# Moving a bank read to another engine, and two residual sums to later places, in a kernel bound by TensorE

## The chip, the cores and the metric

The kernel runs on one core of a Trainium2 chip. The metric is the device time of one execution in microseconds, the median of several runs. Looks of one run: of those, only places are compared. The five instruction streams are TensorE (PE), VectorE (DVE), ScalarE (ACT), GpSimd (POOL) and the DMA issuing queue (SP).

## The reference

A graph attention net on 128 graphs of 64 tokens with 768 features, two layers, in float32:

```python
h = jnp.maximum(_layernorm(x, axis=-1), 0.0)
for l in range(2):
    m_left  = einsum('bsh,oh->bso', h, W_left[l]);  m_right = einsum('bsh,oh->bso', h, W_right[l])
    u_left  = einsum('bih,bjh->bij', h, m_left) / sqrt(768);  u_right = ... m_right ...
    u = u_left * upper_triangle(adj) + u_right * lower_triangle(adj)     # cut: how the masks are made
    e = exp(u) * adj
    attention = e / (sum(e, axis=2) + 1e-10)
    h_lin = einsum('bsh,oh->bso', h, W_lin[l]) + b_lin[l]
    h = relu(layer_norm(attention @ h_lin, ln_a[l], ln_b[l]))
return x + h
```

## The kernel before

The work goes through 16 blocks of 512 tokens. Each 768x768 projection is cut into blocks of 256 and done with 15 block products instead of 18, of sums of token blocks (`ts`) and sums of weight blocks. A product is made in one of the PSUM banks X, Y, Z, V and added to one or two of six output blocks in `hl` (three of 256 columns, for two halves of the tokens), with a sign; further products then accumulate **on top of it in the same bank**. So a bank must be read before the next matmuls of that bank may start: a late read stops TensorE, in the profile of before for 0.45 us at one read and 1.07 at another.

```python
# product i: (weights, bank, tokens, what it is added to)
ORDER = ((5, "X", "ta", "+2"), (8, "Z", "u1", "-0+2"), (0, "X", "u2", "+3"), (1, "Y", "u3", "-3"),
         (12, "X", "B3", "-5"), (6, "V", "B0", "-2"), ...                       # cut
         (3, "X", "u0", "+1-3"), (11, "Y", "te", "+0"), (13, "V", "tc", "-1"), (9, "Z", "tg", "+4"),
         (14, "V", "tf", "+5"))

def read(p, to, i, seen):
    what = ORDER[i][3]
    for n in range(0, len(what), 2):
        sign, o = what[n], int(what[n + 1])
        if o not in seen:                     # first time for this output: a copy, on ScalarE
            seen.add(o)
            nc.scalar.activation(to(o), p, AF.Copy, scale=1.0 if sign == "+" else -1.0)
        else:                                 # else an addition, on VectorE
            added(nc.vector, to(o), sign, to(o), p)
```

Other work is put at numbered slots of the loop over the products: slots 2i and 2i+1 come before and after the read of product i. The place of an instruction in its own engine's queue is fixed by that; nothing else is. The last block goes through the products twice, for one half of the tokens each. In its first half stand the final sums of the half-block before:

```python
def last_block(u):                                                         # cut
    put(1, lambda: load(1))                                                # rows of x, by DMA
    put(6, lambda: nc.gpsimd.tensor_scalar_mul(rows["-b"], rows["b"], -1.0))
    put(20, lambda: load(0))
    for xs, slot in zip(XS[u, 1], (22, 40)):                               # "offset sums": x + b
        put(slot, lambda xs=xs: nc.gpsimd.tensor_add(xs, xs, rows["b"]))

def finish(u, r):                                                          # cut
    # scaled(k): normalise on VectorE, then the "bias sum" on GpSimd
    nc.gpsimd.tensor_add(zs[k], zs[k], rows["b"])
    # done(k): the "residual sum" on VectorE, then the output
    nc.vector.scalar_tensor_tensor(xs[k], zs[k], 0.0, xs[k], op0=ALU.max, op1=ALU.add)

# slots of (inverse, scaled 0, scaled 1, done 0, done 1), for the two half-blocks before
ends = ({0: ((u - 1, 0), (12, 13, 15, 19, 21)), 9: ((u - 1, 1), (28, 29, 30, 39, 41))}, ...)
```

I call the product on "u0" (bank X), the start of the part of interest, **T**: after it come Y, V, Z and the last V group.

The softmax here doesn't subtract the row's maximum and nothing guards it: scores larger than these inputs give would overflow.

Of the kernel before, what the change touches and what calls it, by code (L numbers as in the profile page):

```python
# [17 lines left out]
def kernel(  # L18
# [24 lines left out]
    nc = tc.nc  # L43
# [33 lines left out]
    def put(slot, *fs):  # L77
        plan.setdefault(slot, []).extend(fs)

    def put_all(slot, fs, step=1):  # L80
        for f in fs:
            if f is not None:
                put(slot, f)
            slot += step
        return slot

    def run(slot):
        if slot in plan:
            for f in plan.pop(slot):
                f()  # L90
        elif idle:
            f = idle.popleft()
            if f is not None:
                f()
# [59 lines left out]
    def added(eng, o, sign, a, b):  # L154
        (eng.tensor_add if sign == "+" else eng.tensor_sub)(o, a, b)  # L155
# [13 lines left out]
    def tokens_of(key):  # L169
        ht = HT[key]  # L170
        r = {f"B{2 * j + t}": ht[:, j * K2:(j + 1) * K2, t * TH:(t + 1) * TH] for j in range(3) for t in range(2)}
        r.update(TS.get(key, {}))
        return r
# [12 lines left out]
    def put_sums_t(key, first, step, base):  # L186

        fs = sums_t(key)
        put_all(first, fs[:5], step)
        for f, s in zip(fs[5:], (21, 22, 23, 24, 25, 27)):  # L190
            put(max(base + s, first + 5 * step), f)

    def read(p, to, i, seen):

        what = ORDER[i][3]
        for n in range(0, len(what), 2):
            sign, o = what[n], int(what[n + 1])
            if o not in seen:
                seen.add(o)
                nc.scalar.activation(to(o), p, AF.Copy, scale=1.0 if sign == "+" else -1.0)  # L200
            else:
                added(nc.vector, to(o), sign, to(o), p)
# [60 lines left out]
    def load_h(which, l, u):  # L263
        ht = HT[which, l, u] = big.tile([P, C, T], F32, name="ht")
        nc.sync.dma_start(ht, KEPT[l][u])

    def affine(which, l, u, step=1):

        def part(c0):
            for c in range(c0, c0 + step):  # L270
                ht = HT[which, l, u][:, c, :]
                nc.scalar.activation(ht, ht, AF.Relu, bias=cols[1][:, c:c + 1], scale=cols[0][:, c:c + 1])  # L272

        return [lambda c=c: part(c) for c in range(0, C if l else 0, step)]
# [336 lines left out]
    def fresh(l, i, rs):  # L611

        bank = ps_st.tile([P, 2 * TH], F32, name=FIRST[i][0])
        b = bank.rearrange("p (r d) -> p r d", r=2)[:, :len(rs)]
        if i in PRELOAD:
            nc.scalar.copy(b, rows["bias", l][:, PRELOAD[i]].unsqueeze(1).to_broadcast([P, len(rs), D]))
        return b


    def pass_two(l, aside):  # L620
        last = l == L - 1
        with tc.tile_pool(name=f"two{l}", bufs=2, reuse_waits="tile") as sp:
# [8 lines left out]
            def load_at(u):  # L631
                AT[u] = sp.tile([P, Q, S], F32, name="at", bufs=2)
                nc.sync.dma_start(AT[u], ATT[l][u])
# [37 lines left out]
            def batch(r, k, h):  # L671
                return 4 * (h if k == 0 else 1 - h) + r + 2 * k

            XS = {}

            def last_block(u):


                rest = big.tile([P, C, T], F32, name="ht").rearrange("p c t -> p (c t)")
                rows["-b"] = sp.tile([P, H], F32, name="nb", bufs=1)  # L680
                for r in range(2):
                    XS[u, r] = [rest[:, n * H:(n + 1) * H] for n in (2 * r, 2 * r + 1)]

                def load(r):
                    for k in range(2):
                        for h in range(PAIR):
                            nc.sync.dma_start(XS[u, r][k][h * S:(h + 1) * S], x[u * NBB + batch(r, k, h)])

                put(1, lambda: load(1))
                put(6, lambda: nc.gpsimd.tensor_scalar_mul(rows["-b"], rows["b"], -1.0))  # L690
                put(20, lambda: load(0))
                for xs, slot in zip(XS[u, 1], (22, 40)):
                    put(slot, lambda xs=xs: nc.gpsimd.tensor_add(xs, xs, rows["b"]))

            def finish_last(u, r):
# [120 lines left out]
            def linear(u, rs, base, ends, more):  # L816

                b, w = tokens_of((2, l, u)), W[l, "n"]
                if rs[0] == 0:
                    HL[u] = sp.tile([P, Q, H], F32, name="hl", bufs=2)  # L820
                hl, seen = HL[u], set()
                bank = {"X": AHEAD.pop()}
                early = {0: 3, 2: 5, 6: 9}
                for i, (s, at, t, _) in enumerate(ORDER):
                    if i in FIRST and i not in PRELOAD:
                        bank[at] = fresh(l, i, rs)
                    p = bank[at]
                    for n, r in enumerate(rs):
                        for c in range(K2):
                            nc.tensor.matmul(p[:, n], b[t][:, c, r * P:(r + 1) * P], w[s][:, c, :],  # L830
                                             start=(i in FIRST and i not in PRELOAD and n == c == 0),
                                             stop=(c == K2 - 1), skip_group_check=True)
                        if n == 0:
                            run(base + 2 * i)
                    read(p, lambda o: hl[:, o % 2 * 2 + rs[0]:o % 2 * 2 + rs[0] + len(rs), o // 2 * D:(o // 2 + 1) * D],
                         i, seen)
                    if i in early:
                        bank[FIRST[early[i]][0]] = fresh(l, early[i], rs)
                    if i == 11 and more and 12 not in ends:
                        AHEAD.append(fresh(l, 0, more))  # L840
                    if i in ends:
                        what, slots = ends[i]
                        if slots:
                            for f, n in zip(finish(*what), slots):
                                put(n, f)
                        else:
                            finish_block(what, more)
                    run(base + 2 * i + 1)
# [3 lines left out]
            for u in range(NB):  # L852
                turn = not last and u >= NB - 2
                put(4, lambda u=u: load_at(u))
                if u + 1 < NB:
                    load_h(2, l, u + 1)
                    put_all(9 if u else 15, affine(2, l, u + 1))
                    put_sums_t((2, l, u + 1), 15 if u else 21, 1, 0)
                    if turn:
                        load_rows(1, 0, sp)  # L860
                        put_all(10, transpose_rows(1, 0, sp), 2)
                    if u in aside:
                        aside[u]()
                    ends = {}
                    if u and last:
                        ends = {0: ((u - 1, 0), (6, 7, 8, 11, 12)), 7: ((u - 1, 1), (20, 21, 22, 30, 30))}
                    elif u > NB - 3:
                        ends = {5: ((u - 1, 0), (16, 17, 18)), 11: ((u - 1, 1), (28, 29, 30))}
                    elif u:
                        ends = {12: (u - 1, None)}  # L870
                    linear(u, (0, 1), 0, ends, (0, 1) if u + 2 < NB else (0,))
                    for n in sorted(plan):
                        plan[n - 30] = plan.pop(n)
                else:
                    if turn:
                        load_h(1, 1, 0)
                        put_all(28, affine(1, 1, 0), 3)
                        put_sums_t((1, 1, 0), 38, 2, 30)
                        ends = ({1: ((u - 1, 0), (13, 14, 16)), 11: ((u - 1, 1), (34, 35, 36))},
                                {4: ((u, 0), (50, 51, 52))})  # L880
                    else:
                        last_block(u)
                        ends = ({0: ((u - 1, 0), (12, 13, 15, 19, 21)), 9: ((u - 1, 1), (28, 29, 30, 39, 41))},
                                {2: ((u, 0), (44, 48, 51, 61, 62))})
                    linear(u, (0,), 0, ends[0], (1,))
                    linear(u, (1,), 30, ends[1], ())
                    for n in sorted(plan):
                        run(n)
                    for f in (finish_last if last else finish)(u, 1):
                        f()  # L890
# [48 lines left out]
```

## Time and profile before

| | before |
|---|---|
| median of the first three runs | 2760.3 us (2755.51 to 2762.19) |
| span of the profiled run | 2755.1 us |
| TensorE busy | 2726.7 us, 99% |
| TensorE's own waits together | about 18 us, 8.9 of them at the start |
| first layer, last block: "u2" group to the V group after "B3" | 3.41 us (2.69 at its own pace) |
| second layer, last block: T to the end of the last matmul | 23.0 us |

A row of a timeline has its start, its duration, the engine, the source line, the operation, output and inputs and their shapes, and in brackets the idle time before it and who ended it. Starts of TensorE's groups are more telling than durations, since matmuls overlap: groups of four, 1.03 us long, start 0.86 us apart at its own pace.

### The profile page before, as it was taken

What the parts mean: (1) busy time and instruction counts of PE and PEld (TensorE: products, weight loads), DVE (VectorE), ACT (ScalarE), POOL (GpSimd) and SP (SyncE); (2) the same over time, 40 slices, a digit from 0 to 9 for tenths busy, and PEclk for the clock granted to TensorE, in tenths of its full rate; (3) what the DMA queues carried; (4) which work ended last, traced back from release to release, by engine and by line L of the source; (5) the groups of instructions that cost most, each with busy time, mean ns of one, the idle gap of its engine ahead of it and who ended that gap; (6) DMA issues with size and microseconds to landing.
All of it is one profiled execution on the core that took longest, in us unless ns stands there. A gap on an engine that the chain in (4) does not pass through costs nothing.

```text
span 2755.1 us, 46372 instructions
## 1 busy us (share of the span) xinstructions
PE 2726.7 (99%) x18712; PEld 2339.0 (85%) x18712; DVE 1349.0 (49%) x2268; ACT 850.0 (31%) x1612; POOL 1192.1 (43%) x935
## 2 busy tenths in 40 slices
PE   8999999999999999999999999999999999999998
PEld 7888888888888888888788888888888888888886
DVE  6455455545454333333335444444444335676667
ACT  3222223222221154444621211121122214444443
POOL 3432352224223555555522344223222325887885
PEclk9999999999999999999999999999999999999999
DMA  6534433343332333343555433443344204555655
GB/s 195 129 75 97 121 83 81 86 120 94 76 77 75 102 105 119 119 150 123 148 127 149 101 75 76 108 118 79 76 98 120 59 26 145 160 170 166 175 161 146
DMA packets 234072, 310.82 MB, mean 113 GB/s; under 512 B 54146, under 2 KB 184450, under 8 KB 225666
## 3 DMA queue, kind: packets, MB, share of 16 engines
q1 hardware_dynamic: 233698, 307.45, 41.7%
q8 instruction: 149, 2.44, 0.4%
q14 instruction: 65, 0.53, 0.1%
q10 hardware_dynamic: 160, 0.39, 0.0%
HBM read 202.91 MB, written 104.86 MB: 112 GB/s over the span
## 4 chain that ended last, share of the span: by engine, by line
PE 96%; DVE 1%; DMA 1%; ACT 1%; issue 0%; SPq 0%; DVEq 0%; ACTq 0%
PE X L426 23%; PE V L426 16%; PE X L830 12%; PE Y L426 12%; PE Z L426 8%; PE V L830 8%; PE Y L830 6%; PE aux L453 5%; PE Z L830 4%; PE aux L645 2%; PE aux L668 1%; PE Y L668 0%; ACT ht L272 0%; DMA w_r<-in_w_right_dram 0%; DMA ht<-h 0%
## 5 line engine op out<-in xcount | busy, mean ns | idle before, releaser
L155 POOL TENSOR_TENSOR ts<-ht 128x512 f32<-128x512 f32 x441 | 586.8, 1340 | 1223.1 <-DMA ht<-h 531.1
L200 ACT ACTIVATE m<-X 128x512 f32<-128x512 f32 (+1 forms) x256 | 151.6, 592 | 1086.4 <-PE X L426 570.7
L155 POOL TENSOR_TENSOR ts<-ht,ts 128x512 f32<-128x512 f32 x189 | 248.8, 1323 | 135.1 <-PE X L830 60.5
L155 DVE TENSOR_TENSOR m<-m,V 128x512 f32<-128x512 f32 (+1 forms) x256 | 173.3, 677 | 269.4 <-PE V L426 269.2
L155 DVE TENSOR_TENSOR m<-m,X 128x512 f32<-128x512 f32 (+1 forms) x256 | 162.9, 677 | 249.3 <-PE X L426 248.7
L830 PE MATMUL X<-w_n,ts 128*128 128x256 f32 x1024 | 244.3, 380 | 0.9 <-ACT hl L200 0.6
L426 PE MATMUL X<-ts,w_l 128*128 128x256 f32 x1024 | 242.7, 380 | 0.1
L426 PE MATMUL X<-ts,w_r 128*128 128x252 f32 (+1 forms) x1024 | 238.7, 376 | 0.0
L155 DVE TENSOR_TENSOR m<-m,Z 128x512 f32<-128x512 f32 (+1 forms) x128 | 87.5, 683 | 306.5 <-ACT m L200 246.9
L830 PEld LDWEIGHTS X<-w_n,ts 128*128 128x128 f32 x1024 | 191.4, 190 | 33.4 <-issue 3.7
L426 PEld LDWEIGHTS X<-ts,w_l 128*128 128x128 f32 x1024 | 191.9, 190 | 30.2 <-DVE m L155 2.7
L426 PEld LDWEIGHTS X<-ts,w_r 128*128 128x128 f32 x1024 | 191.9, 190 | 26.1
L272 ACT ACTIVATE ht<-ht,b_col,a_col 128x512 f32<-128x512 f32 x192 | 143.6, 804 | 149.3 <-DMA ht<-h 149.3
L830 PE MATMUL Y<-w_n,ts 128*128 128x256 f32 x768 | 182.5, 379 | 0.0
L426 PE MATMUL Y<-ts,w_l 128*128 128x256 f32 x768 | 181.5, 379 | 0.5 <-DVE w_l L155 0.5
L426 PE MATMUL Y<-ts,w_r 128*128 128x252 f32 (+1 forms) x768 | 179.2, 376 | 1.3 <-POOL w_r L155 1.3
L426 PEld LDWEIGHTS Y<-ts,w_l 128*128 128x128 f32 x768 | 145.8, 190 | 20.7 <-DVE w_l L155 0.9
L830 PEld LDWEIGHTS Y<-w_n,ts 128*128 128x128 f32 x768 | 145.8, 190 | 20.4 <-issue 0.6
L426 PEld LDWEIGHTS Y<-ts,w_r 128*128 128x128 f32 x768 | 145.8, 190 | 19.1 <-POOL w_r L155 1.7
L155 DVE TENSOR_TENSOR hl<-hl,V 128x512 f32<-128x512 f32 (+1 forms) x136 | 89.1, 655 | 129.7 <-PE V L830 112.4
L200 ACT ACTIVATE hl<-X 128x512 f32<-128x512 f32 (+1 forms) x136 | 78.3, 576 | 221.4 <-PE X L830 218.6
L796 POOL TENSOR_TENSOR z<-z,b 128x768 f32<-128x768 f32 x62 | 112.0, 1817 | 79.7 <-DVE z L793 79.7
(162 smaller groups left out, 4730.9 us busy)
## 6 DMA issues: line engine op xcount, KB each, us to landing
ht<-h SPq DMA_DIRECT2D x63, 1536.0 KB, 7.2
h<-xb SPq DMA_DIRECT2D x124, 384.0 KB, 6.1
z<-z SPq DMA_DIRECT2D x128, 192.0 KB, 3.1
x<-z SPq DMA_DIRECT2D x128, 192.0 KB, 8.6
x<-in_x_dram SPq DMA_DIRECT2D x120, 192.0 KB, 8.6
xr<-in_x_dram SPq DMA_DIRECT2D x120, 192.0 KB, 3.7
out_dram<-xr SPq DMA_DIRECT2D x120, 192.0 KB, 2.7
adj<-in_adj_dram SPq DMA_DIRECT2D x64, 128.0 KB, 2.8
```

The source lines that it names most:

```text
L155: (eng.tensor_add if sign == "+" else eng.tensor_sub)(o, a, b)
L200: nc.scalar.activation(to(o), p, AF.Copy, scale=1.0 if sign == "+" else -1.0)
L272: nc.scalar.activation(ht, ht, AF.Relu, bias=cols[1][:, c:c + 1], scale=cols[0][:, c:c + 1])
L426: nc.tensor.matmul(p[:, g], w[ORDER[i][0]][:, c, g * P:(g + 1) * P], b()[t][:, c, :].rearrange(bs, s=S)[:, :, :ns], start=(new and g == c ...
L453: nc.tensor.matmul(p[h * S + e:h * S + e + 32, q, e:e + 95], ht[:, c, b * S + e:b * S + e + 32], mb[:, e:e + 95], start=(c == 0), stop=(c ...
L645: nc.tensor.matmul(cx[k][i, m, :HH], at[j, q, :], hl[j, q, m * HH:(m + 1) * HH], start=True, stop=True)
L668: nc.tensor.matmul(parts[r, k][n][i], at[j, q, :], hl[j, q, cut], start=True, stop=True)
L796: nc.gpsimd.tensor_add(zs[k], zs[k], rows["b"])
L830: nc.tensor.matmul(p[:, n], b[t][:, c, r * P:(r + 1) * P], w[s][:, c, :], start=(i in FIRST and i not in PRELOAD and n == c == 0), stop=(c ...
```

## The change

The intent is to take away two stops of TensorE: the read of "u2" in the last block of the first layer goes from a busy ScalarE to an idle VectorE, and in the last block the residual sums go to later slots, so that they do not stand ahead of the reads of X, with the offset sums on GpSimd put behind them.

```diff
-    def read(p, to, i, seen):
+    def read(p, to, i, seen, copied=nc.scalar):
@@
                 seen.add(o)
+                if copied is nc.vector:
+                    nc.vector.tensor_scalar_mul(to(o), p, 1.0 if sign == "+" else -1.0)
+                    continue
                 nc.scalar.activation(to(o), p, AF.Copy, scale=1.0 if sign == "+" else -1.0)
@@ last_block
-                for xs, slot in zip(XS[u, 1], (22, 40)):
+                for xs, slot in zip(XS[u, 1], (26, 45)):
@@ linear
-                         i, seen)
+                         i, seen, nc.vector if (len(rs), rs[0], i) == (1, 0, 2) and not last else nc.scalar)
@@
-                        ends = ({0: ((u - 1, 0), (12, 13, 15, 19, 21)), ...
+                        ends = ({0: ((u - 1, 0), (12, 13, 15, 22, 24)), ...
```

The changed kernel has three more source lines: L200, L693, L796, L807, L830 of before are L203, L696, L799, L810, L833 there. The new read is L201.

More of the change, by code (lines that the diff above doesn't have):

```diff
@@ L882, in pass_two @@
                         last_block(u)
-                        ends = ({0: ((u - 1, 0), (12, 13, 15, 19, 21)), 9: ((u - 1, 1), (28, 29, 30, 39, 41))},
+                        ends = ({0: ((u - 1, 0), (12, 13, 15, 22, 24)), 9: ((u - 1, 1), (28, 29, 30, 39, 41))},
                                 {2: ((u, 0), (44, 48, 51, 61, 62))})
```

## The prediction

"Lock", here and in the expectations, is the word for what the durations show and for nothing more: the residual sum on VectorE took 0.94 us with GpSimd idle and 2.42 and 1.91 us when a sum on GpSimd was running, and ended some 0.82 us after that one.

> **What bounds the kernel now.** I read the page's busy shares first, then the chain that ended last, then the list of TensorE's own waits, and last the timelines of two short stretches.
>
> ```profile
> PE 2726.7 (99%) x18712; PEld 2339.0 (85%) x18712; DVE 1349.0 (49%) x2268; ACT 850.0 (31%) x1612; POOL 1192.1 (43%) x935
> PE 96%; DVE 1%; DMA 1%; ACT 1%; issue 0%; SPq 0%; DVEq 0%; ACTq 0%
> ```
>
> TensorE is busy 99% of the span and carries 96% of the chain that ended last. Busy matmul time alone would be a weak argument, but the starts are evenly spaced: groups of four 128x256 matmuls begin 0.86 to 0.87 us apart all through the trace, so between the gaps there is nothing for another engine to take away. What can be won is the time in which TensorE stands still for somebody, and that is listed:
>
> ```profile
> PE aux L347 <- ACT x L297: 8.9, 1, 8.9
> PE X L426 <- DVE w_l L155: 1.5, 1, 1.5
> PE Y L426 <- POOL w_r L155: 1.3, 1, 1.3
> ...
> PE V L830 <- DVE hl L155: 1.1, 1, 1.1
> PE X L830 <- ACT hl L200: 1.0, 3, 0.5
> ```
>
> Columns: who waited for whom, us in total, times, longest. Everything here is some 18 us, half of it the start-up. The change addresses two entries: the 1.1 us for one VectorE read of bank V, and the largest of the three waits for a ScalarE read of bank X. The first is in the last block of the second layer, the second in the last block of the first layer. The first layer's place:
>
> ```profile
> 1348.23 1.03 PE L830 MATMUL Y<-w_n,ts 128*128 128x256 f32 x4
> 1349.71 1.13 PE L830 MATMUL X<-w_n,ht 128*128 128x256 f32 x4 [0.45 <-ACT hl L200]
> ...
> 1348.16 0.81 ACT L783 ACTIVATE z<-aux 128x768 f32<-128x768 f32 x1
> ...
> 1349.29 0.36 ACT L200 ACTIVATE hl<-X 128x256 f32<-128x256 f32 x1
> ```
>
> The product "u2" (begun at 1347.26, finished about 1348.39) lies in bank X, and the matmuls on "B3" go on top of it, so it must be read first. The reader is ScalarE, which is busy with two row-square sums and a root until 1349.38; TensorE stands from 1349.26. The second layer's place, VectorE first, then GpSimd, then TensorE:
>
> ```profile
> 2720.62 2.42 DVE L807 SCALAR_TENSOR_TENSOR xr<-z,xr 128x768 f32<-128x768 f32 x1
> 2722.97 0.74 DVE L155 TENSOR_TENSOR hl<-hl,X 128x256 f32<-128x256 f32 x2
> 2723.63 1.91 DVE L807 SCALAR_TENSOR_TENSOR xr<-z,xr 128x768 f32<-128x768 f32 x1
> 2725.46 0.41 DVE L155 TENSOR_TENSOR hl<-hl,Y 128x256 f32<-128x256 f32 x1
> 2725.79 0.41 DVE L155 TENSOR_TENSOR hl<-hl,V 128x256 f32<-128x256 f32 x1
> ...
> 2718.65 3.58 POOL L796 TENSOR_TENSOR z<-z,b 128x768 f32<-128x768 f32 x2 [0.27 <-DVE z L793]
> 2722.78 1.94 POOL L693 TENSOR_TENSOR ht<-ht,b 128x768 f32<-128x768 f32 x1 [0.55 <-DMA ht<-in_x_dram]
> ...
> 2726.35 1.10 PE L830 MATMUL V<-w_n,ts 128*128 128x256 f32 x4 [1.07 <-DVE hl L155]
> ```
>
> The same residual sum (L807) takes 2.42, then 1.91 us here, and 0.94 us where GpSimd is idle (the one at 2735.41). Each long one ends about 0.82 us after a GpSimd sum does: the second bias sum ends at 2722.23, the residual sum at 2723.05; the offset sum (L693) ends at 2724.72, the residual sum at 2725.54. And the offset sum itself took 1.94 instead of 1.82, having started while the first residual sum was running. So the two engines exclude each other. The read of V comes behind both residual sums, and TensorE pays.
>
> [...] the reads of banks X, Y and V take 0.41 us under a running GpSimd sum as well as without. [...]
>
> **The change part by part.** The instruction order of the two kernels, compared engine by engine, differs in few places. TensorE and GpSimd have the same instructions in the same order with the same kinds of wait. ScalarE loses one read and VectorE gains one (first layer). In the last block VectorE's order goes from "sum, X, X, sum, Y, V, Z" to "X, X, sum, Y, sum, V, Z". On the DMA queue the second load of residual rows moves ahead of an output.
>
> 1. First layer's read on VectorE. VectorE has been idle since about 1346.75, so it can begin when bank X is done, about 1348.4. I take 0.42 us for it, as for its other 128x256 reads: free at about 1348.8. TensorE's next start at its own pace is 1348.23 + 0.86 = 1349.09, so the wait goes entirely. Worth: 1349.71 - 1349.09 = 0.62 us, and the group after a stop takes 0.96 to the next start (1350.67) instead of 0.86, which is 0.10 more. Sum: -0.72 us. Later waits in that block are for things that TensorE itself paces (reads of banks made just before), so they move along and give nothing back.
>
> 2. Offset sums "behind". GpSimd's queue is unchanged: bias sum, bias sum, offset sum, in that order. The first offset sum waits only for its rows (idle 0.55 us, ended by the DMA). A later place in the program does not hold it, since no other instruction stands between on GpSimd and it waits on nothing of VectorE. It should start at about 2722.78 as before, on before's clock, and so should the second, behind the two bias sums. Worth: 0.
>
> 3. Residual sums later. On before's clock. The reads of X wait for their matmuls (2721.56 + 1.13 = 2722.69), begin at about 2722.75 and end two starts of 0.33 later, at 2723.4. The first residual sum now comes up at 2723.4 with the offset sum holding the lock since 2722.78, for 1.82: until 2724.6. It ends 0.82 later, at 2725.42. Y: issued at 2725.34, the next start 0.33 later. Second residual sum from 2725.67, lock free, 0.94: next start about 2726.53. The read of V therefore begins at 2726.53, where it began at 2725.79: +0.74. TensorE started V 0.56 after the read began (2726.35 - 2725.79); it now starts at about 2727.09. Worth: +0.74 us. All of that is on the path, because the rest of this block, the last context and the closing chain of VectorE hang on TensorE's pace.
>
> The loss follows from one plain fact: before, the first residual sum spent its lock wait in time when VectorE had nothing else to do (X was not yet ready). Moved behind X, it meets the offset sum instead, while the second sum still stands ahead of V.
>
> 4. Earlier load of rows: they are used some 20 us later. Worth: 0.
>
> Sum: -0.72 + 0 + 0.74 + 0 = about 0.0 us of 2755.
>
> **The rivals.** (a) What the change is meant to do: if the offset sum fell behind both residual sums, they would take 0.94 each: 2723.4, Y, 2724.6, V at about 2725.5, and TensorE's stop shrinks by some 0.3 us; with step 1 about -1 us. With the stop gone altogether (own pace 2724.25 + 0.86 = 2725.11, so 1.24 + 0.1) it is -2 us. Against it: GpSimd's unchanged order and waits. For it: the load could land later, as more loads follow it closely. (b) The residual sum wins the lock and the offset sum comes between it and the second one: 2723.4 to 2724.3, offset sum to about 2726.0, second sum to 2726.85, V at 2726.8: +1.0 instead of +0.74, in all +0.3 us. It needs the rows to land 0.6 us later than before. (c) The moved read in the first layer delays VectorE's other reads. [...] the next one (Y) waited until 1349.69 in any case, for ScalarE's read; it will come earlier. I give that little weight. All rivals lie within -2 to +1 us, under a tenth of a percent.
>
> **Range and chances.** The three timed runs before lie 6.7 us apart (2755.51 to 2762.19, median 2760.3), and the profiled one took 2756.92. That scatter is larger than every branch above. So I predict 2760.0 us, with 2755 to 2764 for 8 in 10, that is the scatter of before plus the branches. 2% would be 55 us, and all waits of TensorE together are some 18: faster 0.005, same 0.99, slower 0.005.
>
> **What would show it.** Step 1: TensorE's 0.45 us wait before the "B3" matmuls of the first layer's last block is gone and the bank X read stands on VectorE at about 0.4 us. Step 2: GpSimd's first offset sum begins right after its rows land, not behind the residual sums. Step 3: the first residual sum shows about 2.0 us, the second about 0.95, and TensorE's stop before the last V group grows from 1.07 to about 1.8 us. It is wrong if that stop shrinks, if the offset sum starts after 2724, or if another wait of TensorE over 0.3 us appears. The time as a whole would be wrong only if a new wait repeated in all blocks, and nothing changes in them.

## The result, and the profile after

The changed kernel took 2758.66 us (median of 4 runs, 2756.18 to 2759.05), the kernel before 2758.3 (median of 4, the three above and one more). The ratio is 0.9998 with a 95% interval from 0.9981 to 1.0016: the same. A ratio is the mean time of one kernel's runs over that of the other's of the same rounds, so not quite the ratio of the medians. Busy times hardly differ:

```profile
PE 2726.2 (99%) x18712; PEld 2339.2 (85%) x18712; DVE 1347.4 (49%) x2269; ACT 849.5 (31%) x1611; POOL 1192.3 (43%) x935
```

TensorE's waits (us in total, times, longest) show what this hides. The 0.45 us wait for ScalarE's read is gone; the one that the second part was made for has doubled:

```profile
PE aux L350 <- ACT x L300: 8.6, 1, 8.6
PE V L833 <- DVE hl L155: 2.1, 1, 2.1
PE X L833 <- ACT X L619: 1.7, 1, 1.7
...
PE X L833 <- ACT hl L203: 0.6, 2, 0.3
```

The first layer's place in the changed kernel, TensorE, then VectorE:

```profile
1347.66 1.03 PE L833 MATMUL Y<-w_n,ts 128*128 128x256 f32 x4
1348.53 1.03 PE L833 MATMUL X<-w_n,ht 128*128 128x256 f32 x4
...
1347.86 0.42 DVE L201 TENSOR_SCALAR hl<-X 128x256 f32<-128x256 f32 x1 [1.68 <-PE X L833]
```

The read (L201) takes 0.42 us on VectorE after 1.68 us of idleness, and "B3" starts at TensorE's pace, 0.87 us after the group before it, where it was 1.48. And the last block, VectorE, GpSimd, TensorE:

```profile
2723.98 0.95 DVE L810 SCALAR_TENSOR_TENSOR xr<-z,xr 128x768 f32<-128x768 f32 x1
2724.85 0.41 DVE L155 TENSOR_TENSOR hl<-hl,Y 128x256 f32<-128x256 f32 x1
2725.18 2.23 DVE L810 SCALAR_TENSOR_TENSOR xr<-z,xr 128x768 f32<-128x768 f32 x1
2727.34 0.41 DVE L155 TENSOR_TENSOR hl<-hl,V 128x256 f32<-128x256 f32 x1
...
2724.51 2.09 POOL L696 TENSOR_TENSOR ht<-ht,b 128x768 f32<-128x768 f32 x1 [1.76 <-DMA ht<-in_x_dram]
...
2724.77 1.03 PE L833 MATMUL Z<-w_n,ts 128*128 128x256 f32 x4
2727.89 1.10 PE L833 MATMUL V<-w_n,ts 128*128 128x256 f32 x4 [2.10 <-DVE hl L155]
```

The first residual sum came up 1.91 us after T (2722.07) and found GpSimd idle: 0.95 us. But the offset sum began 2.44 us after T, in the middle of it, and so stood first in line when the second residual sum came up at 3.11 us. That one waited for the end of the offset sum (2726.60) and ended 0.81 us later. The read of V, behind it, started 1.55 us later than in the kernel before on the common clock, or 1.04 after allowing for the different T. Why the offset sum began so much later than before (1.23 us after T there) is not told by one trace.

The third line of the waits, 1.7 us, is new too. It lies at the start of the second layer's second pass and hangs on the landing of a 1.5 MB load; in the fourteen profiles, this wait was between 0.16 and 1.73 us, and 0.16, 0.23 and 1.55 for three looks at one and the same program. It is scatter, and no part of the change.

### The profile page after: what moved, and what is told of

Read it like the earlier page. It is cut to its first block, busy times and chain, and to the rows that moved or that the text cites. A ratio compares the mean times of both kernels' runs of the same rounds, so it can differ in the third digit from the quotient of the medians.

```text
span 2756.7 us, 46373 instructions
## 1 busy us (share of the span) xinstructions
PE 2726.2 (99%) x18712; PEld 2339.2 (85%) x18712; DVE 1347.4 (49%) x2269; ACT 849.5 (31%) x1611; POOL 1192.3 (43%) x935
## 3 DMA queue, kind: packets, MB, share of 16 engines
q8 instruction: 149, 2.44, 0.4%
## 5 line engine op out<-in xcount | busy, mean ns | idle before, releaser
L203 ACT ACTIVATE m<-X 128x512 f32<-128x512 f32 (+1 forms) x256 | 151.5, 592 | 1086.0 <-PE X L429 570.1
L833 PE MATMUL X<-w_n,ts 128*128 128x256 f32 x1024 | 244.3, 380 | 2.5 <-ACT X L619 1.7
L833 PEld LDWEIGHTS X<-w_n,ts 128*128 128x128 f32 x1024 | 191.5, 190 | 35.0 <-issue 3.1
L833 PE MATMUL Y<-w_n,ts 128*128 128x256 f32 x768 | 182.5, 379 | 0.0
L833 PEld LDWEIGHTS Y<-w_n,ts 128*128 128x128 f32 x768 | 145.8, 190 | 20.4 <-issue 0.6
L203 ACT ACTIVATE hl<-X 128x512 f32<-128x512 f32 (+1 forms) x135 | 77.9, 577 | 222.2 <-PE X L833 219.3
L799 POOL TENSOR_TENSOR z<-z,b 128x768 f32<-128x768 f32 x62 | 111.9, 1816 | 79.4 <-DVE z L796 79.4
```

Of the source, the lines that this page charges most:

```text
L833: nc.tensor.matmul(p[:, n], b[t][:, c, r * P:(r + 1) * P], w[s][:, c, :], start=(i in FIRST and i not in PRELOAD and n == c == 0), stop=(c ...
```

## The experiments

My theory: the two parts are independent, each worth what it does to one local wait; in the last block all that counts is whether GpSimd is in the middle of a sum when a residual sum comes up (0.94 us if not, 1.9 to 2.4 if so, in the profile of before). Rivals: the moved read costs something later; the order of loads or the offset sums' places matter; the stop is due to the mere number of sums ahead of V.

Each kernel was profiled once. From each trace I took five starts, and worked out: the distance from the Z group to the last V group (0.86 at TensorE's pace), the start of the offset sum after T, the durations of the two residual sums, the time from T to the end of the last matmul, and the time at half clock in between. Behind the last matmul every kernel needs another 10.5 to 10.6 us.

| run | first-layer read | sums | Z to V | offset sum after T | residual sums | T to last matmul | half clock |
|---|---|---|---|---|---|---|---|
| before | ScalarE | old | 2.10 | 1.23 | 2.42, 1.91 | 23.0 | 0 |
| e3_offsets_only (= before) | ScalarE | old | 1.14 | 2.71 | 2.43, 0.95 | 22.0 | 0 |
| t_same_program (= before) | ScalarE | old | 1.13 | 2.07 | 2.42, 0.95 | 22.0 | 0 |
| e1_first_read_only | VectorE | old | 1.14 | 2.46 | 2.43, 0.94 | 22.1 | 0 |
| t_first_read | VectorE | old | 1.14 | 3.17 | 2.43, 0.95 | 22.1 | 0 |
| after | VectorE | new | 3.12 | 2.44 | 0.95, 2.23 | 24.0 | 0 |
| r_after | VectorE | new | 3.12 | 2.00 | 0.95, 2.23 | 25.7 | 3.41 |
| e2_sums_only | ScalarE | new | 3.16 | 2.76 | 0.95, 2.27 | 25.7 | 3.41 |
| t_sums | ScalarE | new | 3.12 | 2.28 | 0.95, 2.23 | 24.0 | 0 |
| e4_rows_in_old_order | VectorE | new | 3.12 | 2.18 | 0.95, 2.23 | 25.7 | 3.41 |
| e5_held_behind | VectorE | new | 1.84 | 4.26 | 0.95, 0.95 | 23.1 | 0 |
| e6_second_sum_after_z | VectorE | other | 0.86 | 2.54 | 2.43, 1.07 | 22.3 | 0 |
| e7_longer_stop | VectorE | new | 5.38 | 2.68 | 0.95, 0.95 | 28.8 | 6.83 |
| e8_first_read_held | VectorE | old | 1.14 | 3.23 | 2.43, 0.95 | 22.1 | 0 |

In the first layer the distance from "u2" to V was 3.41 or 3.42 us in all five looks with ScalarE, and 2.69 or 2.70 in all nine with VectorE.

### The parts alone

**e1_first_read_only** keeps the first part and undoes the others:

```diff
-                for xs, slot in zip(XS[u, 1], (26, 45)):
+                for xs, slot in zip(XS[u, 1], (22, 40)):
-                        ends = ({0: ((u - 1, 0), (12, 13, 15, 22, 24)), ...
+                        ends = ({0: ((u - 1, 0), (12, 13, 15, 19, 21)), ...
```

> Only the first layer's read moves to VectorE; the last block is as before. My theory (two independent local waits): TensorE's 0.45 us wait before the B3 matmuls of the first layer's last block is gone, and from the start of the u2 group to the start of the V group it takes 2.70 us instead of 3.41; the last block keeps its stop of 1.07 us and its residual sums of about 2.4 and 1.9 us. Rival (the read costs VectorE time that comes back later): a new wait of TensorE over 0.3 us in the 30 us behind the moved read. The whole time cannot tell: 0.7 us lies under the scatter of 6.7 us.

The first layer came as expected: 2.69 us, no wait. No new wait followed, so the rival falls. But the stop in the last block was not 1.07 us: it was 0.12, with a residual sum of 0.94 where I expected 1.9. The order there was that of before; so the profile of before was not typical of its own order.

**e2_sums_only** keeps the later residual sums and undoes the others:

```diff
-                for xs, slot in zip(XS[u, 1], (26, 45)):
+                for xs, slot in zip(XS[u, 1], (22, 40)):
-                         i, seen, nc.vector if (len(rs), rs[0], i) == (1, 0, 2) and not last else nc.scalar)
+                         i, seen)
```

> Only the residual sums of the last block move (the offset sums keep their old places in the program, the read stays on ScalarE). My theory (what counts is who holds the lock when a sum comes up, and GpSimd's order never changed): the 0.45 us wait in the first layer is there, and the last block shows what the whole change showed: one residual sum of about 0.95 and one of 1.9 to 2.3 us, a stop of TensorE before the last V group of 1.8 us if the rows land at the old distance, 2.1 us if they land late. Rival (moving the offset sums is a part of it): the stop comes out clearly different, under 1.5 or over 2.4 us.

As the theory had it: sums of 0.95 and 2.27 us and a stop of 2.13 us, without any change of the offset sums' places. From T to the last matmul it took 25.7 us, though, 1.7 more than the changed kernel with the same stop. That I had not expected, and come back to.

**e3_offsets_only** moves the offset sums alone. It builds to the same instructions in the same order on every engine as the kernel before:

```diff
-                for xs, slot in zip(XS[u, 1], (22, 40)):
+                for xs, slot in zip(XS[u, 1], (26, 45)):
```

> Only the places of the offset sums move. Compared instruction by instruction this program has the same instructions, order and kinds of wait as the kernel before on every engine, so it is a second look at the kernel before. My theory: stop of 1.07 us (to 0.2) before the last V group, residual sums around 2.4 and 1.9 us, first layer's wait 0.45 us. If the landing of the rows scatters from run to run, as I believe, the start of the offset sum after TensorE's group on u0 (1.22 us before, 2.44 after the change) may differ here too, with the same program. Rival (the late landing comes from the changed order of loads): 1.22 us within 0.2 again.

So the third part of the change is none: a later slot only changes an instruction's place among those of its own engine, and on GpSimd nothing stood between. The stop was 0.11 us and not 1.07, with the same program. The rows landed late, 2.71 us after T.

**e4_rows_in_old_order** is the change with the next load put back behind the outputs, as it stood on the queue before:

```diff
-                put(20, lambda: load(0))
+                put(23, lambda: load(0))
```

> The whole change, but the second load of residual rows is put back behind the first pair of outputs, so that the queue's order is again that of the kernel before. Theory A (the rows landed late because the next load follows on them closely): the offset sum starts about 1.2 us after TensorE's group on u0 again, holds the lock when the first residual sum comes up, residual sums of about 2.0 and 0.95 us, stop of TensorE 1.8 us, as my prediction had it. Theory B (the late landing is scatter of the transfers): the start of the offset sum lies anywhere between 1.2 and 2.5 us after that group, and the stop between 1.8 and 2.1 us follows from it.

The offset sum still began 2.18 us after T: theory B. The order of loads is not what makes the rows late. Of 12 looks in which nothing holds the offset sum back, one had it at 1.23 us and eleven between 2.00 and 3.17; the odd one is the profile on which I had based the prediction.

A second look at the kernel before (**t_same_program**, below) shows how the usual case goes. VectorE, GpSimd, TensorE:

```profile
2723.60 0.95 DVE L810 SCALAR_TENSOR_TENSOR xr<-z,xr 128x768 f32<-128x768 f32 x1
2724.46 0.41 DVE L155 TENSOR_TENSOR hl<-hl,Y 128x256 f32<-128x256 f32 x1
2724.80 0.41 DVE L155 TENSOR_TENSOR hl<-hl,V 128x256 f32<-128x256 f32 x1
...
2723.59 2.62 POOL L696 TENSOR_TENSOR ht<-ht,b 128x768 f32<-128x768 f32 x1 [1.40 <-DMA ht<-in_x_dram]
...
2725.35 1.10 PE L833 MATMUL V<-w_n,ts 128*128 128x256 f32 x4
```

The second residual sum comes up 2.08 us after T. If the offset sum is not yet under way by then, the residual sum takes 0.95 us, here with GpSimd as the one held off (2.62 us instead of 1.81), and V is read in time. It was close: the two start within 0.01 us of each other. In the old order both residual sums have begun before the rows usually land; in the new order the second one comes up at 3.11 us, by which time they usually have landed.

### Is it the two engines' exclusion?

**e5_held_behind** adds to the change one tiny copy on GpSimd that reads the result of the second residual sum. It makes the offset sum really follow:

```diff
+                put(25, lambda: nc.gpsimd.tensor_copy(stat.tile([P, 1], F32, name="hold", bufs=1), XS[u - 1, 0][1][:, :1]))
```

> The whole change plus one 128x1 copy on GpSimd that reads the second residual sum's result and stands ahead of the first offset sum, so that the offset sum really lies behind the residual sums. Lock theory: both residual sums take about 0.95 us, the read of V comes about 4.0 us after the start of the group on u0 (5.3 with the change), TensorE's stop is about 0.8 to 0.9 us instead of 2.1, and the clock stays full. Rival (the stop comes from the two sums standing ahead of V as such, the lock is a side matter): the stop stays at 1.8 us or more.

VectorE, then GpSimd:

```profile
2723.38 0.95 DVE L811 SCALAR_TENSOR_TENSOR xr<-z,xr 128x768 f32<-128x768 f32 x1
2724.25 0.41 DVE L155 TENSOR_TENSOR hl<-hl,Y 128x256 f32<-128x256 f32 x1
2724.58 0.95 DVE L811 SCALAR_TENSOR_TENSOR xr<-z,xr 128x768 f32<-128x768 f32 x1
2725.45 0.41 DVE L155 TENSOR_TENSOR hl<-hl,V 128x256 f32<-128x256 f32 x1
2726.11 1.46 DVE L792 TENSOR_SCALAR rs<-sd 128x2 f32<-128x2 f32 x1
...
2725.60 0.18 POOL L695 COPY hold<-xr 128x1 f32<-128x1 f32 x1 [3.44 <-DVE xr L811]
2725.73 1.81 POOL L697 TENSOR_TENSOR ht<-ht,b 128x768 f32<-128x768 f32 x1
```

Both sums take 0.95 us and the stop falls from 2.1 to 0.82 us, as expected. So of the changed kernel's stop 1.28 us are the exclusion, and 0.8 us remain because two sums stand between the reads of X and V at all. It is still worse than the old order's 0.1: even the intended version of the second part would not have paid in the usual case.

The wait is not quite to the other's end plus the full duration: a residual sum in the changed kernel ended 0.81 us after GpSimd's instead of the 0.95 it takes alone, and the offset sum of t_same_program (2.62 us, with a residual sum ending 0.96 us after its start) needed 1.66 of its 1.81 afterwards. Nor was it only large instructions that waited: above, the one of 128x2 (L792) took 1.46 us, to 0.03 us after GpSimd's sum had ended, where it takes 0.16 with GpSimd idle (at 2726.46 in before).

### The half clock

**r_after** is the changed kernel again, **e7_longer_stop** the changed kernel with four needless multiplications ahead of the second residual sum:

```diff
+                for _ in range(4):
+                    put(24, lambda: nc.vector.tensor_scalar_mul(rows["-b"], rows["-b"], 1.0))
```

A window, below and in the expectation of e7, is a stretch of 3.41 us, the length of the half clock in e2 and e4.

> The changed kernel once more, for the scatter of its places. If the stop before the last V group is a property of the order, it is 1.8 to 2.3 us again, whenever the rows land. [...]

> The whole change plus four multiplications by 1.0 of a 128x768 row tile on VectorE ahead of the second residual sum[...], results unchanged. It makes TensorE's stop about 2 us longer, some 4 us[...]. [...] the clock is at half for one window, perhaps two, right behind. Rival (the half clocks seen in two of four runs had another cause): the clock stays full after a stop twice as long.

In r_after the stop was again 2.09 us, from 2725.29 to 2727.38, and the groups behind it were slow. TensorE's groups, and then a table of two windows of 3.41 us (stretch, its length, busy time and count of PE, weight loads, DVE, ACT and POOL, granted clock, DMA share, GB/s):

```profile
2727.38 1.10 PE L833 MATMUL V<-w_n,ts 128*128 128x256 f32 x4 [2.09 <-DVE hl L155]
2728.32 1.77 PE L833 MATMUL X<-w_n,ts 128*128 128x256 f32 x4
2729.88 1.91 PE L833 MATMUL Z<-w_n,ts 128*128 128x256 f32 x4
2731.59 1.18 PE L833 MATMUL X<-w_n,ts 128*128 128x256 f32 x4
...
2725.05:2728.46 3.41, 1.32 (x7) 1.00 (x6) 2.76 (x5) 0.00 (x0) 1.04 (x1) 1.00 0.84 251
2728.46:2731.88 3.42, 3.42 (x10) 2.71 (x9) 2.27 (x3) 0.71 (x3) 1.86 (x2) 0.50 0.98 261
```

The half clock lasted 3.41 us in r_after, e2 and e4 and 6.83 in e7; in the traces that have a half step, its edges give the grid, and in the others I continue the grid from the edge where the clock falls after the last matmul (in the traces of before and after, the full clock lasted 2734.08 and 2737.49 us up to that edge, 801 and 802 times 3.413). In r_after TensorE was busy for 1.32 us of the window that holds the stop, 39%, and the next window ran at clock 0.50. In e2_sums_only it was 1.38 us and in e4 1.35, both 40%, and the same followed. In the changed kernel's first profile an edge of the grid cut the stop in two, and the two windows had 2.37 and 2.35 us busy. In t_sums the worse of the two had 1.94 us, 57%. Neither lost the clock:

```profile
2726.68:2730.10 3.42, 1.94 (x9) 1.76 (x10) 2.71 (x7) 0.00 (x0) 0.19 (x1) 1.00 0.96 285
```

e7 made the stop 4.35 us and got two windows at half clock, 6.83 us, behind windows with 0.77 and 1.71 us busy (23% and 50%). The ends of the programs, where no stop is at work, agree: t_same_program's last window with matmuls had 1.47 us busy, 43%, and the next one ran at half clock; the changed kernel's had 2.21 us, 65%, and the next one kept the clock. So in these runs the half clock came behind windows with TensorE busy for 50% or less, and behind none that I looked at with 57% or more; whether the stop leaves such a window goes by where it falls on the grid. That the busy share decides is my reading of these few cases. The half clock costs 1.7 us: 25.7 instead of 24.0 us from T to the last matmul. Three of the five looks at the new order without a hold had it.

### The whole time

Three timings of five rounds, all on one chip: the two parts alone, and the kernel before against itself.

> The first layer's read alone, timed. From the profiles: 0.7 us saved, and the last block as before, that is from the start of the u0 group to the end of the last matmul 22.1 us when the rows land late (two of three looks at that order) or 23.0 when early. Theory: ratio to the kernel before 0.9995 to 0.9999, 0.2 to 1.5 us less; the interval may well include 1. Rival (the change as a whole is neutral because its first part gains nothing real): 1.0000 with no lean to either side.

> The later residual sums alone, timed. From the profiles: the last block takes 24.0 us from the u0 group to the last matmul without a half clock, 25.7 with one, instead of 22.1 to 23.0. Theory: 1 to 3.6 us slower than the kernel before, ratio 1.0004 to 1.0013, most probably about 1.001. Rival (they cost 0.7 us, as my prediction had it from one profile): ratio under 1.0004. The profile shows the stop of 2.1 us again [...].

> The offset sums' places alone, which give the same program as before, timed as a measure of what five rounds can tell: ratio 1.0000, off by at most 0.0005. The profile is a fourth look at the old order of the last block: a stop of 0.1 to 0.3 us if the rows land later than about 2 us after the start of the u0 group, about 1.1 us if they land before the second residual sum comes up.

| kernel, 5 runs each | median us | lowest to highest | ratio to before | 95% interval |
|---|---|---|---|---|
| t_first_read | 2755.08 | 2753.81 to 2755.76 | 0.9995 | 0.9981 to 1.0008 |
| t_sums | 2758.72 | 2757.22 to 2758.98 | 1.0008 | 0.9995 to 1.0020 |
| t_same_program | 2755.93 | 2753.10 to 2758.16 | 0.9999 | 0.9987 to 1.0012 |
| before, 9 runs of these rounds | 2756.48 | 2754.01 to 2757.29 | | |

Against the kernel before each interval includes 1, so none of these is shown by time alone. Against each other the two parts are apart: every run of the later sums was slower than every run of the first read, by 3.4 us in the mean (2758.21 and 2754.81). The places say 0.7 us for the read and 2.0 us, or 3.7 with the half clock, for the sums, together 2.7 to 4.4. t_sums's profile had no half clock. The changed kernel again, in r_after's rounds: 2757.89 us (2754.42 to 2759.63), ratio 1.0005, from 0.9993 to 1.0018, against 2755.95 for before.

### Two versions meant to beat both

**e6_second_sum_after_z** keeps the first part, leaves the first residual sum where it was, and puts the second behind the reads of V and Z:

```diff
-                        ends = ({0: ((u - 1, 0), (12, 13, 15, 22, 24)), ...
+                        ends = ({0: ((u - 1, 0), (12, 13, 15, 19, 27)), ...
```

> A version that is to beat both: the first layer's read on VectorE, the first residual sum where it was before, the second behind the reads of V and Z (slot 27), the offset sums as before. Then no sum stands between the reads of X and V, whoever holds the lock. Theory: TensorE's start of the last V group comes 0.86 to 0.90 us after the Z group, no stop over 0.15 us in that block, no wait in the first layer's, no half clock in the closing block. A later wait of the second sum may reach the next sums, but not TensorE. Time: 1 to 3 us under the changed kernel, which the scatter may hide. Rival (the later sum delays the loads and sums of the next half and gives the time back): a wait of TensorE over 0.3 us later in the block, or the closing chain ends later relative to the last matmul.

The Z to V distance was 0.86 us, TensorE's own pace, but what was won there was given back: the next context product came 0.36 us sooner after T than in t_first_read (7.10 and 7.46 us), while the normalising pass, which frees its banks, came 0.24 us later (5.68 and 5.44). So the weight loads of that product waited 0.38 us for the pass, and the product (L648) took 2.01 us to the next group instead of 1.45:

```profile
2727.73 2.08 PE L648 MATMUL aux<-hl,at 64*64 64x384 f32 x16
2729.74 1.13 PE L833 MATMUL Y<-w_n,ts 128*128 128x256 f32 x4
```

The rival was right in effect: 0.36 us won up to the product, 0.56 lost in it, 22.3 us instead of 22.1. The median of five was 2753.70 us, the ratio 0.9992 (0.9978 to 1.0005).

**e8_first_read_held** keeps the first part and the old order, and adds the hold, to take away the case of early rows:

```diff
+                put(22, lambda: nc.gpsimd.tensor_copy(stat.tile([P, 1], F32, name="hold", bufs=1), XS[u - 1, 0][1][:, :1]))
```

> A second candidate to beat both: the first layer's read on VectorE, the residual sums in their old places, and the 128x1 copy on GpSimd that makes the first offset sum wait for the second residual sum. It takes away the one case in which the old order was slow (rows landing before the second residual sum comes up). Theory: stop before the last V group about 0.1 us, second residual sum about 0.95 us, offset sum starting after it (3.0 us or more after the start of the u0 group), 22.0 to 22.1 us from there to the last matmul's end, full clock; first layer 2.69 us. Time 0.5 to 2 us under the kernel before. Rival: the offset sum, held, now runs into the next bias sums and the last block takes over 22.3 us.

All places came as expected: stop 0.11 us, offset sum 3.23 us after T, 22.1 us to the last matmul, full clock. The median was 2753.71 us (2753.64 to 2757.30) against 2755.62, ratio 0.9993 (0.9979 to 1.0006). So e6 and e8 are the lowest medians; by their places they beat both kernels, by time against the kernel before it is not shown. Since the rows landed late in this look anyway, the hold's gain in the early case is argued from the order and not seen.

## Why the prediction was right or wrong

The whole time was predicted at 2760.0, with 2755 to 2764, and came at 2758.66: right, because the scatter is larger than everything that the change does. The range was the scatter, so that this number tests nothing of the mechanism. The steps:

- **Step 1, the first layer's read: right.** 3.41 to 2.69 us is -0.72, the predicted sum of 0.62 and 0.10, in all looks. The duration of 0.42 us was right too, and nothing was given back.
- **Step 2, the offset sums: the mechanism right, the start wrong.** They are not behind anything, and e3 shows that their part of the diff changes no instruction. But the step went on: "It should start at about 2722.78 as before". That took the landing of rows in one profile for a property of the program. In eleven of twelve looks it came 0.8 to 1.9 us later. By its own test ("if the offset sum starts after 2724") this step failed: 2724.51. Its third sign, another wait of TensorE over 0.3 us, came too (1.7 us at the start of the second layer's second pass), but that one is scatter, as shown above.
- **Step 3, the residual sums: the sign right, the term mis-sized.** The stop grew, but the first sum was the short one and the second the long one, the reverse of what I had; this is rival (b), whose +1.0 us over the profiled kernel before is what came (24.0 instead of 23.0). And the base was unusual: the old order's usual stop is 0.1 us. Against that, the later sums cost 2.0 us (24.0 against 22.0), not 0.74.
- **A term that the sum lacked:** the half clock, 1.7 us more in three of five looks. No step had it.
- **Step 4, the earlier load: right,** as far as seen. Its place moved no landing that could be told from scatter (e4).
- **The sum of "about 0.0 us" was wrong as a property of the two orders:** in the usual case it is -0.72 + 1.98 = +1.3 us, with the half clock +3.0. It happened to stay hidden in the scatter of 7 us. Rival (a) was tried by e5: both sums at 0.95 us and a stop of 0.8 us, which is what it forecast for the case, but still no gain over the usual old order. Rival (c) was rightly given little weight. One reading was too strict: in the same trace some groups start 0.95 to 0.97 us apart (2713.78 to 2714.73), not 0.86 to 0.87 "all through"; nothing rests on it.

What stays open is why the rows land when they do. The load is issued in four pieces. In the profile of before the issue of the second piece took 0.60 us and in that of the changed kernel 1.65, with the same queue ahead of it. But in e3 it took 0.60 us as well, and the offset sum still began 2.71 us after T; so this alone does not explain the late rows, and what sets them from run to run I have not tried to find.

## What to carry to other kernels

Before a stop seen in one trace is worth an edit, look at the same program twice more: of the two waits that this change set out to remove, the larger one was there in one of three looks, the other in all. A later place in the program holds an instruction back only behind others of its own engine (e3: later slots, the same program); to order two engines that hold each other off, as these sums did, give them a data dependency; a one-column copy was enough here (the offset sum began 4.26 us after T in e5 and 3.23 in e8, behind both residual sums). And a short stop of TensorE can cost nearly twice its length: behind the one of 2.1 us the clock was at half for 3.41 us in three of five looks, which cost 1.7 us more.
